# The first two heads of a cross-attention and feed-forward kernel in true fp32 products

## The chip, the cores and the metric

The kernel runs on one core of one Trainium2 chip. The metric is the device time of one execution in microseconds, the median of the runs shown. Durations come from one profiled execution; their times are counted from the start of its span.

## The reference

Two residual blocks follow one another on `x` of shape (2, 512, 512), fp32. Cut to what matters:

```python
h    = layernorm(x)
q_hk = (h @ Wq.T).reshape(B, S, 16, 128)                # "down"
q_big = einsum('bshk,hkq->bshq', q_hk, w_kc_q)          # "up", 384 wide
q_big = q_big * cos + rotate_half(q_big) * sin
q_r  = einsum('bshq,hqr->bhsr', q_big, W_qr)            # rank 64
k_r  = einsum('bld,hdr->bhlr', rope(ctx), W_kr)         # ctx: (2, 1024, 128)
attn = softmax(q_r @ k_r.T)
x    = x + ((attn @ rope(ctx)) @ w_kc_kv.T).reshape(B, S, 2048) @ Wo.T
y    = layernorm(x)
x    = x + bit_linear(silu(bit_linear(y, gate)) * bit_linear(y, val), out)
```

`bit_linear` rounds its input to 8-bit levels and its weight to -1, 0, 1 times a mean. All inputs are fp32. The scores are sharp, so the chain from `h` to `q_r` has to keep more than a 16-bit product gives.

## The kernel before, in words

The attention runs in 32 steps `i`, one for a head and a batch. `STEPS` orders them: step 0 is head 0 of batch 0, step 1 head 1 of batch 0, steps 2 and 3 the same heads of batch 1, then heads 2 and 3, and so on. A weight is prepared once for a head `u` and serves two steps.

Precision is kept by pairs of parts. The weight of a head (`rawa`, 128 rows, 896 columns of down and up weights and 192 of the rank projection) is scaled by a power of two and split into two fp16 parts, `whi` and `wlo`. The normalized input `hid` is turned by TensorE and split into two fp16 parts (`hid_part`). A product is then three fp16 matmuls: high by high, high by low, low by high. In front of the split stand `w_mass` (a bound on the weight's size), `w_bound` (a matmul that spreads it over the partitions), `w_factor` (the power of two), `w_scale`, `w_hi`, `w_lo`. For the first two heads (`FIRST = 2`) ScalarE does the mass, the scaling and the high part; for the others VectorE and GpSimd do. The rank weight is split into two parts of the reduced fp32 type `F32R` (`wr_hi`, `wr_lo`) that lie side by side.

A step passes through these functions:

- `q_down`: four chunks of the 512-wide contraction, three fp16 matmuls each (L603), into one PSUM bank.
- `q_hi` (ScalarE, L610) and `q_lo` (VectorE, L614): the two fp16 parts of the result.
- `q_up`: three blocks of 128 columns, three fp16 matmuls each (L622).
- `rot_copy`, `rot_half` (ScalarE), `rot_cos` (VectorE), `rot_sin`, `rot_add` (GpSimd): the rotation.
- `rot_hi` (ScalarE, L646) and `rot_lo` (GpSimd, L650): two F32R parts of each rotated block.
- `q_rank`: three blocks, two F32R matmuls each (L657). The two halves of its output hold the products with the high and the low part of the rank weight.
- `t_hi` twice (ScalarE, L665), `t_res` (L671) and `t_lo` (L676, both VectorE): the query in two F32R parts, scaled back.
- `score` (L717), `s_max` (L721), `s_exp` (L725), `s_scale`, `s_recip`, `e_hi` (L737), `e_lo` (L742), `e_turn` (a transposing DMA), `mix` (L757), `project` (L775): scores, softmax, weighted context and output.

Beside the steps run the table and context work of the start (`kv_*`, `val_*`, `load_*`), the keys (`key_*`), and the quantization of the feed-forward weights (`w_sum`, `w_round`, `w_tern`, `w_store`), which reads its input twice. The feed-forward stage (`ff_*`) follows when attention ends; its weights lie in buffers with the tags `ffg` and `ffv`, which nothing else uses before.

The order of all work is written out by hand in the table `ISSUE`: each function has a tuple of places, one for each call. The calls are sorted by place and issued in that order, and each engine, the DMA queue of SyncE included, works through its own instructions strictly in it. Before the first real work, TensorE runs idle products of an identity (L464, fp32, 12 of them) and of a wide tile (L470).

Of the kernel before, what the change touches and what calls it, by code (L numbers as in the profile page):

```python
# [13 lines left out]
F32 = mybir.dt.float32  # L14
# [19 lines left out]

HIDS = 2.0 ** 10

FIRST = 2


def qscale(u):  # L40
    return 2.0 ** -14 if u < FIRST else 2.0 ** -16
# [18 lines left out]
        528, 577, 582, 537, 766, 775, 761, 745, 962, 1087, 1050, 994, 1164, 1175, 1198, 1213, 1450, 1418, 1479, 1411,  # L60
        1623, 1626, 1598, 1573, 1879, 1869, 1806, 1823, 2030, 2002, 2013, 2059, 2293, 2272, 2306, 2373, 2501, 2464,
        2524, 2476, 2727, 2718, 2647, 2774, 2849, 2857, 2907, 2932, 3102, 3131, 3044, 3050, 3298, 3236, 3284, 3229,
        3353, 3356, 3397, 3411, 3487, 3505, 3526, 3538,
    ),
    "b_hi": (144, 220, 533, 784, 876, 1189, 1405, 1645, 1883, 2046, 2266, 2509, 2770, 2862, 3079, 3270),
    "b_lo": (163, 226, 556, 798, 892, 1190, 1413, 1658, 1934, 2065, 2342, 2516, 2771, 2872, 3100, 3272),
    "c_hi": (
        402, 489, 649, 729, 859, 948, 1077, 1151, 1261, 1358, 1446, 1537, 1679, 1783, 1913, 1983, 2145, 2228, 2374,
        2418, 2547, 2623, 2757, 2835, 2936, 3021, 3139, 3220, 3324, 3344, 3426, 3483,
    ),  # L70
    "c_lo": (
        408, 490, 662, 731, 866, 950, 1080, 1152, 1276, 1378, 1470, 1538, 1703, 1797, 1914, 1988, 2187, 2246, 2375,
        2420, 2548, 2628, 2758, 2836, 2937, 3022, 3150, 3223, 3325, 3345, 3475, 3484,
    ),
    "e_hi": (
        225, 258, 280, 300, 324, 352, 394, 407, 476, 442, 500, 535, 562, 586, 611, 631, 645, 663, 706, 739, 759, 772,
        797, 826, 847, 870, 905, 927, 951, 982, 997, 1028, 1048, 1076, 1097, 1123, 1142, 1179, 1202, 1211, 1240, 1262,
        1311, 1326, 1361, 1399, 1407, 1440, 1445, 1491, 1507, 1535, 1559, 1582, 1616, 1646, 1666, 1687, 1725, 1768,
        1764, 1831, 1834, 1872, 1884, 1942, 1943, 1994, 2023, 2042, 2091, 2095, 2128, 2134, 2182, 2202, 2249, 2242,
        2295, 2297, 2332, 2349, 2390, 2400, 2426, 2450, 2478, 2507, 2530, 2557, 2580, 2602, 2627, 2650, 2684, 2710,  # L80
        2723, 2754, 2780, 2794, 2841, 2843, 2889, 2913, 2931, 2994, 3009, 2973, 3053, 3043, 3095, 3086, 3126, 3144,
        3178, 3204, 3226, 3241, 3253, 3286, 3306, 3312, 3346, 3366, 3385, 3395, 3423, 3437,
    ),
    "e_lo": (
        236, 265, 285, 310, 329, 353, 404, 409, 480, 445, 501, 545, 572, 587, 612, 633, 654, 685, 720, 740, 760, 778,
        811, 830, 857, 877, 911, 931, 960, 983, 998, 1032, 1054, 1078, 1098, 1124, 1144, 1180, 1203, 1222, 1246, 1263,
        1312, 1343, 1375, 1400, 1416, 1461, 1463, 1505, 1508, 1536, 1565, 1585, 1619, 1654, 1673, 1689, 1735, 1772,
        1771, 1835, 1837, 1877, 1890, 1945, 1949, 2007, 2024, 2045, 2092, 2096, 2131, 2161, 2186, 2203, 2253, 2250,
        2296, 2298, 2333, 2362, 2391, 2404, 2427, 2469, 2482, 2508, 2535, 2558, 2591, 2608, 2638, 2653, 2691, 2715,
        2732, 2755, 2795, 2800, 2855, 2856, 2892, 2922, 2934, 3006, 3015, 2976, 3065, 3054, 3111, 3087, 3127, 3165,  # L90
        3183, 3210, 3228, 3242, 3279, 3287, 3308, 3320, 3349, 3375, 3389, 3399, 3425, 3441,
    ),
    "e_turn": (
        257, 276, 336, 337, 373, 374, 454, 457, 486, 532, 522, 546, 664, 665, 690, 691, 704, 719, 747, 750, 777, 782,
        831, 848, 858, 878, 930, 932, 987, 1007, 1038, 1052, 1075, 1079, 1137, 1181, 1194, 1214, 1223, 1299, 1308,
        1309, 1350, 1376, 1448, 1449, 1466, 1520, 1499, 1550, 1553, 1570, 1649, 1667, 1683, 1717, 1753, 1754, 1786,
        1827, 1858, 1859, 1870, 1880, 1908, 1946, 1987, 2100, 2055, 2056, 2102, 2139, 2152, 2194, 2221, 2263, 2264,
        2365, 2307, 2336, 2385, 2402, 2424, 2425, 2444, 2521, 2540, 2541, 2565, 2594, 2617, 2667, 2701, 2707, 2742,
        2744, 2769, 2773, 2817, 2822, 2881, 2897, 2903, 2986, 2999, 3080, 3083, 3099, 3113, 3114, 3137, 3153, 3181,
        3187, 3193, 3256, 3277, 3278, 3288, 3289, 3334, 3342, 3372, 3386, 3390, 3400, 3463, 3464,  # L100
    ),
    "ff_center": (3378, 3368, 3434, 3438, 3521, 3520, 3567, 3570),
    "ff_end": (3677, 3725, 3809, 3766, 3847, 3854, 3862, 3865),
    "ff_gate": (
        3443, 3447, 3460, 3469, 3516, 3522, 3534, 3498, 3573, 3555, 3547, 3586, 3620, 3609, 3594, 3629, 3649, 3658,
        3666, 3641, 3692, 3717, 3707, 3674, 3737, 3760, 3723, 3759, 3777, 3791, 3797, 3824,
    ),
    "ff_hint": (
        3513, 3515, 3539, 3540, 3600, 3623, 3601, 3619, 3636, 3668, 3679, 3655, 3698, 3701, 3699, 3713, 3720, 3770,
        3732, 3788, 3787, 3807, 3790, 3795, 3818, 3823, 3819, 3822, 3840, 3841, 3845, 3849,  # L110
    ),
    "ff_hmax": (
        3479, 3481, 3486, 3488, 3563, 3564, 3565, 3572, 3603, 3616, 3617, 3631, 3656, 3663, 3664, 3670, 3680, 3704,
        3710, 3712, 3728, 3731, 3754, 3755, 3769, 3773, 3782, 3785, 3813, 3821, 3832, 3836,
    ),
    "ff_hround": (
        3502, 3506, 3508, 3509, 3576, 3611, 3575, 3618, 3635, 3667, 3678, 3637, 3693, 3684, 3691, 3705, 3718, 3746,
        3730, 3784, 3761, 3757, 3758, 3792, 3808, 3806, 3804, 3820, 3838, 3839, 3844, 3843,
    ),
    "ff_hscale": (3501, 3574, 3634, 3675, 3715, 3756, 3786, 3837),  # L120
    "ff_hturn": (3541, 3646, 3727, 3742, 3799, 3810, 3825, 3842, 3850),
    "ff_in": (
        3435, 3436, 3445, 3446, 3448, 3450, 3458, 3459, 3503, 3504, 3510, 3511, 3518, 3523, 3492, 3493, 3557, 3558,
        3553, 3554, 3535, 3542, 3584, 3585, 3599, 3602, 3589, 3590, 3587, 3588, 3615, 3622, 3647, 3648, 3652, 3653,
        3654, 3665, 3639, 3640, 3688, 3689, 3711, 3716, 3696, 3697, 3669, 3673, 3734, 3735, 3743, 3745, 3721, 3722,
        3736, 3741, 3762, 3763, 3779, 3783, 3774, 3775, 3802, 3803,
    ),
    "ff_int": (3404, 3406, 3473, 3490, 3559, 3597, 3628, 3671),
    "ff_max": (3379, 3382, 3439, 3452, 3530, 3531, 3591, 3592),
    "ff_out": (  # L130
        3560, 3577, 3578, 3581, 3685, 3695, 3702, 3703, 3729, 3789, 3800, 3801, 3748, 3749, 3751, 3752, 3815, 3816,
        3817, 3846, 3828, 3829, 3833, 3834, 3848, 3852, 3853, 3856, 3858, 3859, 3860, 3864,
    ),
    "ff_prod": (
        3462, 3466, 3468, 3472, 3533, 3537, 3546, 3507, 3583, 3571, 3562, 3598, 3626, 3613, 3614, 3633, 3657, 3662,
        3687, 3645, 3706, 3726, 3738, 3683, 3768, 3772, 3767, 3781, 3812, 3814, 3831, 3835,
    ),
    "ff_residual": (3497, 3431, 3500, 3457, 3740, 3851, 3861, 3659),
    "ff_round": (3403, 3402, 3454, 3489, 3552, 3595, 3627, 3621),
    "ff_scales": (3401, 3453, 3536, 3606),  # L140
    "ff_silu": (
        3444, 3449, 3465, 3470, 3532, 3524, 3543, 3499, 3579, 3556, 3561, 3596, 3625, 3610, 3607, 3630, 3650, 3660,
        3686, 3642, 3694, 3724, 3709, 3682, 3744, 3771, 3747, 3780, 3798, 3805, 3811, 3830,
    ),
    "ff_store": (3796, 3753, 3827, 3776, 3857, 3855, 3863, 3866),
    "ff_turn": (3405, 3456, 3474, 3529, 3638, 3604, 3643, 3690),
    "ff_value": (
        3442, 3451, 3461, 3471, 3512, 3527, 3544, 3494, 3582, 3569, 3548, 3593, 3624, 3612, 3605, 3632, 3651, 3661,
        3672, 3644, 3700, 3719, 3708, 3676, 3739, 3765, 3733, 3764, 3778, 3793, 3794, 3826,
    ),  # L150
    "ff_vbias": (3467, 3545, 3549, 3608, 3681, 3714, 3750),
    "hid_norm": (7, 8, 33, 26, 126, 128, 152, 156),
    "hid_part": (25, 27, 36, 37, 46, 47, 41, 42, 138, 154, 140, 146, 167, 168, 177, 183),
    "hid_turn": (9, 24, 45, 31, 130, 129, 159, 176),
    "key_hi": (
        71, 88, 272, 331, 477, 543, 641, 681, 937, 963, 1110, 1125, 1279, 1296, 1427, 1513, 1738, 1775, 1915, 1958,
        2166, 2177, 2352, 2392, 2485, 2578, 2730, 2813, 2992, 3030, 3162, 3200,
# [16 lines left out]
    ),  # L174
    "kv_add": (35, 64, 135, 210),
    "kv_cos": (34, 55, 107, 155),
    "kv_hi": (56, 67, 182, 253),
    "kv_lo": (60, 68, 197, 273),
    "kv_sin": (32, 50, 122, 196),
    "ln_eps": (4, 14, 106, 127),  # L180
# [1095 lines left out]
```

## Time and profile before

| | before |
|---|---|
| median of 3 runs | 776.47 us (775.09 to 776.72) |
| profiled execution, its own time | 773.01 us |
| its span | 771.2 us |
| mean granted TensorE clock | 0.987 |
| TensorE busy | 727.8 us (94%) |
| VectorE busy | 706.4 us (92%) |
| ScalarE busy | 671.5 us (87%) |
| GpSimd busy | 603.0 us (78%) |
| DMA | 145.28 MB, mean 188 GB/s |

An engine's share is an average over the start, the 32 steps and the feed-forward stage. Matmuls are pipelined: a row of the trace gives a 512-column fp16 matmul 0.38 us from start to end, while the next one starts 0.216 us after it. Work on TensorE is counted by the second number.

### The profile page before, as it was taken

What the parts mean: (1) busy time and instruction counts of PE and PEld (TensorE: products, weight loads), DVE (VectorE), ACT (ScalarE), POOL (GpSimd) and SP (SyncE); (2) the same over time, 40 slices, a digit from 0 to 9 for tenths busy, and PEclk for the clock granted to TensorE, in tenths of its full rate; (3) what the DMA queues carried; (4) which work ended last, traced back from release to release, by engine and by line L of the source; (5) the groups of instructions that cost most, each with busy time, mean ns of one, the idle gap of its engine ahead of it and who ended that gap; (6) DMA issues with size and microseconds to landing.
All of it is one profiled execution on the core that took longest, in us unless ns stands there. A gap on an engine that the chain in (4) does not pass through costs nothing. (4 is left out here: it accounts for less than half of the span.)

```text
span 771.2 us, 12603 instructions
## 1 busy us (share of the span) xinstructions
PE 727.8 (94%) x3949; PEld 479.9 (62%) x3958; DVE 706.4 (92%) x1255; ACT 671.5 (87%) x1110; POOL 603.0 (78%) x599
## 2 busy tenths in 40 slices
PE   6767999999999998999999999999999998899998
PEld 5333765666676665666766677777766776553443
DVE  6899999999999898989898999999999999999995
ACT  6698999999998998999999999998898987766873
POOL 3889998788787777898898888897987763379972
PEclk8798999999999999999999999999999999999999
DMA  8635878899999989999999989999999899843354
GB/s 257 204 115 113 187 169 178 192 189 230 209 207 208 226 204 212 213 236 212 214 224 213 207 172 228 198 220 200 201 255 179 183 202 211 157 125 69 69 119 127
DMA packets 326083, 145.28 MB, mean 188 GB/s; under 512 B 291968, under 2 KB 299136, under 8 KB 325760
## 3 DMA queue, kind: packets, MB, share of 16 engines
q1 hardware_dynamic: 326016, 144.48, 85.5%
q8 instruction: 31, 0.51, 0.3%
q14 instruction: 36, 0.29, 0.1%
HBM read 55.31 MB, written 8.39 MB: 83 GB/s over the span
## 5 line engine op out<-in xcount | busy, mean ns | idle before, releaser
L757 PE MATMUL mps<-et,kvh 128*128 128x256 f16 x1024 | 174.8, 273 | 2.2 <-DMA et<-e 1.9
L742 DVE SCALAR_TENSOR_TENSOR e<-sc,m,e 128x1024 f16<-128x1024 f32 x128 | 163.1, 1278 | 8.4 <-ACT e L737 6.9
L721 DVE TENSOR_REDUCE m<-sc 128x1 f32<-128x1024 f32 x128 | 155.4, 1217 | 8.7 <-PE sc L717 7.3
L737 ACT ACTIVATE e<-sc,m 128x1024 f16<-128x1024 f32 x128 | 142.2, 1116 | 17.0 <-ACT sc L725 7.3
L650 POOL TENSOR_TENSOR l<-u,h 128x512 fp32r<-128x512 f32 x96 | 123.8, 1290 | 42.4 <-ACT h L646 25.6
L725 ACT ACTIVATE sc<-sc,m 128x1024 f32<-128x1024 f32 x128 | 139.4, 1089 | 8.2 <-DVE m L721 7.0
L639 POOL TENSOR_TENSOR c<-c,sinq 128x512 f32<-128x512 f32 x96 | 123.5, 1288 | 23.5 <-ACT c L626 13.7
L757 PE MATMUL mps<-et,kvl 128*128 128x256 f16 x512 | 139.6, 273 | 0.0
L642 POOL TENSOR_TENSOR u<-u,c 128x512 f32<-128x512 f32 x96 | 122.7, 1282 | 11.7 <-DVE u L636 6.6
L757 PEld LDWEIGHTS <-kvh 128*128 128x128 f16 x1024 | 94.4, 98 | 40.2 <-issue 20.8
L603 PE MATMUL qps<-hid,whi 128*128 128x512 f16 x256 | 80.6, 397 | 5.5 <-DVE am L967 2.0
L717 PE MATMUL sc<-ko,t 128*128 128x512 f32 x256 | 75.5, 416 | 7.3 <-DVE e L742 2.7
L717 PE MATMUL sc<-ke,t 128*128 128x512 f32 x256 | 75.2, 416 | 4.2 <-DVE e L742 2.5
L636 DVE TENSOR_TENSOR u<-ups,cosq 128x512 f32<-128x512 f32 x96 | 65.2, 681 | 2.9 <-POOL l L650 1.5
L646 ACT CAST h<-u 128x512 fp32r<-128x512 f32 x96 | 59.0, 620 | 4.2 <-POOL u L642 3.8
L717 PEld LDWEIGHTS sc<-ko,t 128*128 128x128 f32 x256 | 44.3, 188 | 26.6 <-issue 4.7
L717 PEld LDWEIGHTS sc<-ke,t 128*128 128x128 f32 x256 | 45.0, 189 | 20.4 <-issue 5.8
L775 PE MATMUL pps<-woh,ch 128*128 128x512 f32 x128 | 54.0, 421 | 0.0
L603 PE MATMUL qps<-hid,wlo 128*128 128x512 f16 x128 | 50.6, 395 | 3.3 <-POOL wlo L554 3.3
L757 PEld LDWEIGHTS <-kvl 128*128 128x128 f16 x512 | 50.1, 98 | 5.7
L775 PE MATMUL pps<-woh,cl 128*128 128x512 f32 x128 | 50.6, 395 | 0.4 <-DVE cl L765 0.3
L775 PE MATMUL pps<-wol,ch 128*128 128x512 f32 x128 | 50.1, 392 | 0.0
(168 smaller groups left out, 1645.9 us busy)
## 6 DMA issues: line engine op xcount, KB each, us to landing
rawa<-in_wall SPq DMA_DIRECT2D x16, 544.0 KB, 4.5
fd<-fo SPq DMA_DIRECT2D x48, 128.0 KB, 3.0
rawb<-in_wall SPq DMA_DIRECT2D x16, 320.0 KB, 3.8
fs<-in_fg SPq DMA_DIRECT2D x16, 256.0 KB, 3.2
ke<-kl SPq DMA_DIRECT2D x32, 128.0 KB, 3.2
ko<-kl SPq DMA_DIRECT2D x32, 128.0 KB, 3.2
ft<-in_fg SPq DMA_DIRECT2D x16, 256.0 KB, 3.4
fs<-in_fv SPq DMA_DIRECT2D x16, 256.0 KB, 3.6
```

What stands on the lines that cost most here:

```text
L603: nc.tensor.matmul(qs[i][0], lhsT=a[:, c * K:(c + 1) * K], rhs=hidp[b][:, m, c, :], start=c == 0 and n == 0, stop=c == 3 and n == 2,)
L636: nc.vector.tensor_tensor(us[i, j], up[i, j], cosq[:, j, :], ALU.mult)
L639: nc.gpsimd.tensor_tensor(cs[i, j], cs[i, j], sinq[:, j, :], ALU.mult)
L642: nc.gpsimd.tensor_tensor(us[i, j], us[i, j], cs.pop((i, j)), ALU.add)
L650: nc.gpsimd.tensor_tensor(ls[i, j], us.pop((i, j)), sb(hs[i, j]), ALU.subtract)
L717: nc.tensor.matmul(ps[:, block(c)], lhsT=a[:, rows], rhs=keys[i][:, block(c)], start=n == 0, stop=n == 1)
L721: nc.vector.tensor_reduce(m[:, 0:1], sc[i, st], AX.X, ALU.max, negate=True)
L725: nc.scalar.activation(ps, ps, AF.Exp, bias=m[:, 0:1], accum_out=m[:, 1:2])
L737: nc.scalar.activation(e[:, 0, :], sc[i, st], AF.Copy, scale=sm[i, st][:, 2:3])
L742: nc.vector.scalar_tensor_tensor(e[:, 1, :], sc.pop((i, st)), m[:, 2:3], e[:, 0, :], ALU.mult, ALU.subtract)
L757: nc.tensor.matmul(ps, lhsT=a[:, b, c, :], rhs=et[:, m + c, :], start=c == 0 and n == 0, stop=c == 7 and n == 2)
L775: nc.tensor.matmul(ps, lhsT=a[:, rows], rhs=w, start=m == 0, stop=m == 5)
```

## The change

For heads 0 and 1, that is for steps 0 to 3 (`FULL = 4`), the chain from the normalized input to the rank projection works on plain fp32 operands:

- `load_a` of these heads loads only the 896 columns of down and up weights, into one fp32 tile with the tag `ffv`. Mass, bound, factor, scaling and split of these two weights are gone.
- `wr_hi` becomes two DMAs that put the rank weight into both halves of an fp32 tile; `wr_lo` is gone for these heads.
- A new step `hid_full` copies each turned block of the input to an fp32 tile with the tag `ffg` (ScalarE, eight calls). The fp16 parts of the input are still made for the other heads.
- `q_down`, `q_up` and `q_rank` issue one fp32 matmul where they issued three, three and two.
- `q_hi` becomes a plain copy; `q_lo`, `rot_hi`, `rot_lo`, the second `t_hi` and `t_lo` are gone in these steps; `t_hi` and `t_res` work on all 128 rows.
- The whole table `ISSUE` is new. The list has 3,825 calls instead of 3,867.

In the diff, cut to its core (the tuples of `ISSUE` are left out):

```diff
 HIDS = 2.0 ** 10
+QS = 2.0 ** -16
 FIRST = 2
-def qscale(u):
-    return 2.0 ** -14 if u < FIRST else 2.0 ** -16
+FULL = 2 * FIRST
...
     def load_a(u):
+        if u >= FIRST:
+            raw[u, 0] = const.tile([P, WB], F32, tag="rawa", name=f"rawa{u}")
+            nc.sync.dma_start(raw[u, 0], wall[SPLITS[u], :, 0:WB])
+            return
+        if not u in wsp:
+            both = const.tile([P, FIRST, WA], F32, tag="ffv", name="rawf")
+            for k in range(FIRST):
+                wsp[k] = [both[:, k, :]]
+        nc.sync.dma_start(wsp[u][0], wall[SPLITS[u], :, 0:WA])
...
     def wr_hi(u):
+        if u < FIRST:
+            w = wsp[u, 2] = wspl.tile([P, 3, 2 * R], F32, tag="wr", name=f"wr{u}")
+            for e in range(2):
+                nc.sync.dma_start(w[:, :, half(e)], wall[SPLITS[u], :, WA:WB].rearrange("p (c r) -> p c r", c=3))
+            return
...
     def q_down(i, c):
+        if i < FULL:
+            w = wsp[SPLIT[i]][0]
+            nc.tensor.matmul(qs[i][0], lhsT=w[:, c * K:(c + 1) * K], rhs=hidf[0][:, b, c, :], start=c == 0, stop=c == 3)
+            return
...
     def q_hi(i):
+        if i < FULL:
+            qs[i].append(lp.tile([P, S], F32, tag="l", name=f"qf{i}"))
+            nc.scalar.copy(qs[i][1], qs[i][0])
+            return
...
     def q_up(i, j):
+        if i < FULL:
+            nc.tensor.matmul(ps, lhsT=wsp[SPLIT[i]][0][:, wc], rhs=qs[i][1], start=True, stop=True)
+            return
...
     def rot_cos(i, j):
-        us[i, j] = up_.tile([P, S], F32, tag="u", name=f"u{i}_{j}")
+        n, tag = (hp, "h") if i < FULL else (up_, "u")
+        us[i, j] = n.tile([P, S], F32, tag=tag, name=f"u{i}_{j}")
...
     def q_rank(i, n):
+        if i < FULL:
+            nc.tensor.matmul(rs[i], lhsT=wsp[SPLIT[i], 2][:, j, :], rhs=us.pop((i, j)), start=n == 0, stop=n == 2)
+            return
...
     def t_hi(i, n):
+        if i < FULL:
+            nc.scalar.copy(ts[i][0], rs[i])
+            return
...
     def t_res(i):
+        if i < FULL:
+            nc.vector.tensor_tensor(ts[i][1], rs[i], sb(ts[i][0]), ALU.subtract)
+            return
...
+    def hid_full(t):
+        if not hidf:
+            hidf[0] = const.tile([P, B, 4, S], F32, tag="ffg", name="hidf")
+        b, cols = t // 4, slice(t % 4 * P, (t % 4 + 1) * P)
+        nc.scalar.copy(hidf[0][:, b, :, cols], hps[t].rearrange("p (c s) -> p c s", c=4))
```

In the new order the first 30 entries of TensorE are: the turns 0, 3, 2, 1, the first key block, `q_down` of step 0, `q_up` of step 0 (with the second key block and one turn of the context among them), `q_down` of step 1, turns 4 and 5, one `q_up` of step 1, the three `q_rank` of step 0 (with turn 7 among them), the rest of `q_up` of step 1, turn 6, the first score. Before, turn 6, turn 7 and two turns of the context stood among or ahead of the same steps. `load_a` of head 0 was the sixth load call of SyncE's queue; it is now the fifteenth, behind seven of the eight blocks of `x` (256 KB each), two blocks of the context with their swapped copies (256 KB each), both tables (512 KB each) and a key weight (64 KB). From the first `mix` on the two orders differ by local exchanges: a call's distance from the end of the list changes by some 15 places on average.

## The prediction

> **What bounds the kernel now.** I read the page first (busy shares, slices), then a table by stages, then the waits of TensorE in the start, then single rows. The page's slices:
>
> ```profile
> PE   6767999999999998999999999999999998899998
> DVE  6899999999999898989898999999999999999995
> PEclk8798999999999999999999999999999999999999
> ```
>
> TensorE is short of work only in the first four slices (77 us) and a little near the end; VectorE is full from the second slice on. The table by stages cuts at the first matmul of `q_down` (16.55 us), at the first usable score (49.5), at the first `mix` (83.0) and near the end of attention (640). The numbers behind an engine are busy us and instructions; behind the last engine stand granted clock, DMA share and GB/s.
>
> ```profile
> core 0: us, PE busy (x) PEld busy (x) DVE busy (x) ACT busy (x) POOL busy (x), PEclk, DMA share, GB/s
> 0.00:16.55 16.55, 11.01 (x61) 9.13 (x61) 10.26 (x39) 11.57 (x19) 3.82 (x13) 0.91 0.86 268
> 16.55:22.14 5.59, 5.34 (x15) 2.10 (x15) 3.95 (x7) 1.30 (x4) 4.68 (x4) 0.64 0.84 295
> 22.14:49.50 27.36, 17.04 (x71) 8.73 (x69) 26.14 (x59) 21.45 (x42) 23.32 (x20) 0.88 0.53 161
> 49.50:83.00 33.50, 27.25 (x111) 15.34 (x112) 32.55 (x53) 30.39 (x54) 30.66 (x26) 0.90 0.48 106
> 83.00:640.00 557.00, 548.46 (x3115) 382.12 (x3114) 516.82 (x824) 520.04 (x866) 455.79 (x419) 1.00 0.97 206
> ```
>
> From 83 to 640 us TensorE works 548.5 of 557 us at full clock: there, time is TensorE's work. Between 22 and 83 VectorE works 58.7 of 60.9 us, and TensorE waits. So the start is worth what VectorE's queue can be shortened by, and a microsecond of TensorE costs something only behind the first `mix`. The waits of TensorE between 16 and 83 us say the same: a late `wlo`, and results of VectorE.
>
> ```profile
> PE rps L657 <- DVE hid L901: 3.3, 1, 3.3
> PE qps L603 <- POOL wlo L554: 3.3, 1, 3.3
> PE sc L717 <- DVE e L742: 2.1, 1, 2.1
> PE qps L603 <- DVE am L967: 2.0, 1, 2.0
> ```
>
> **The change, queue by queue, up to the first `mix`.** I count what each issue list has ahead of the first `mix`, each call at the mean of its row.
>
> *VectorE.* Gone: four `q_lo` of 0.69 (2.8), two of the `t_lo` of 0.75 that stood ahead of that point (1.5), two `w_factor` of three 0.15 us instructions (0.9); three `t_res` at 0.68 instead of 0.75 (0.2). By the new order one `s_max` and one `e_lo` of step 1 fall behind the first `mix` and one `rot_cos` comes ahead of it (1.8). Together 7.2: from 73.0 us to 65.8. The row 73.0 fits the table, whose stages up to 83 us add to 72.9.
>
> *ScalarE.* Gone: mass, scale and high part of two weights (6.2), two `wr_hi` (0.7), 11 `rot_hi` of 0.62 (6.8), three second `t_hi` (2.0), 0.2 on the others, one `e_hi` by order (1.1). Added: eight `hid_full`, at the 0.59 of `hid_part` (4.7), and two `rot_half` by order (1.2). From 70.6 to 59.4.
>
> *GpSimd.* Gone: 11 `rot_lo` of 1.285 (14.1) and `w_lo`, `wr_lo` and the small product of two weights (5.4); one `rot_sin` more. From 66.3 to 48.1.
>
> *TensorE.* Before, a step costs 12 and 9 fp16 matmuls at 0.216 and 6 F32R matmuls at 0.231: 5.9 us. After, it costs ten fp32 products of 512 columns, which this trace does not have. The nearest rows are the idle products at the start, 12 in the code and 24 in the trace:
>
> ```profile
> 1.36 5.49 PE L464 MATMUL warm<-ident 128*128 128x128 f32 x24 [1.36 <-POOL ident masks.py:199]
> ...
> L464 PEld LDWEIGHTS warm<-ident x24: 286/333/333, 1.4 to 6.2; 128*128 128x128 f32 x24
> ```
>
> An fp32 product is two instructions. If each streamed its columns once, a product would cost 2 x 0.231 = 0.46 us; if these rows scale with the columns (5.19 us of loads over 12 products, times 4), 1.73. The median load of such a block takes 333 ns, that of an F32R block of the same size 188 (L717), so I take two passes for each instruction: 4 x 0.216 = 0.86 us, between the ends. The Trainium skill speaks against the change here ("FP8 and Floating Point Precision", TensorE Precision Notes): true fp32 takes four passes where the pairs take three or two. No run here shows that price; by it the sum is the one that I make. Ten products are 8.6 us a step, 2.7 more than before, 10.7 over four steps. Ahead of the first `mix` lie 37 of the 40, and two `w_bound` go: from 39.6 us to 48.9.
>
> **When the first `mix` comes.** *Its beginning does not move.* `load_a` of head 0 now stands behind 4.0 MB instead of 1.3; with its own 0.46 MB, and at the 268 GB/s of the first stage, it lands at 16.6 us, about where `q_down` starts now. The new DMAs, two for each rank weight, stand in SyncE's queue ahead of a context block and two loads; four issues at the 0.5 us of `load_swapped` are 2 us in a queue that was empty from 22.4 to 31.6, and they pass under the rotation of step 0. I cost them at nothing; without that cover it is 2 us.
>
> *The chain of step 0.* At the half clock that the second stage starts with, two products take 1.72 us each, then two 0.86: 5.2 us, against 4.9 now from `q_down` to `q_hi` (21.49). `q_up` has no `q_lo` to wait for, so its first block ends where it does now, near 23.4. Then GpSimd no longer stands in the way: of the 22.7 us that it has ahead of the first `q_rank`, 11.8 go. VectorE has 33.5 us ahead of the first score instead of 38.0, so I expect that score 4.5 us sooner by VectorE alone, and up to 6.5 with less stretching (below).
>
> *The stage.* With VectorE as full as now, the first `mix` comes 7.2 us sooner, at 75.8. For TensorE that leaves 59.2 us from 16.6 on, for 46.6 us of work (48.9 less what lies ahead of `q_down`). It may lose 12.6 us, where it loses 28.6 now (66.5 less 37.9). Of these, 3.3 are the wait for `wlo`, which is gone, and 6.7 half clock (the clock's shortfall times TensorE's busy time in three stages), which denser work shortens.
>
> Two things bound that 7.2. The 1.8 by order are work put off, not saved: at worst they come back, and the shift is 5.4. On the other side VectorE's rows are stretched beside GpSimd's, and GpSimd has 18 us less to do:
>
> ```profile
> 30.38 1.87 DVE L854 SCALAR_TENSOR_TENSOR ln<-ln 128x1 f32<-128x1 f32 x2
> ...
> 64.36 3.96 DVE L938 TENSOR_TENSOR ktl<-kvt,kth 128x512 fp32r<-128x512 f32 x1
> ```
>
> Elsewhere these take 0.23 us for the two and 0.68; GpSimd ran tensor-tensor instructions through both. The four `ktl` rows at a mean of 1.90 give 4.9 us, and the `ln` and `kvt` rows of the start bring it to some 10; a third of that gone would make the shift 10.5.
>
> Behind the first `mix` TensorE has three fp32 products of `q_rank` more, 3 x (0.86 - 0.46) = 1.2 us, at full price. **Sum: -7.2 + 1.2 = -6.0 us.** Against the profiled execution (773.0 us, span 771.2 and 1.8 around it) that is 767.0; the median lies 3.5 above that execution, so 770.5. Own range: -9.3 with less stretching, -4.2 when the order gives nothing, and 1 us for 557 us of shuffled order: 766 to 773.5.
>
> **Rivals.** *TensorE becomes the bound of the start (slower).* It loses 28.6 us now. If only the waits for `wlo` and the 3.3 us wait at the first `rps` go, 22.0 stay, since turns, products and scores stand in one strict queue and each longer product holds up what is behind it. Then the first `mix` comes at 16.6 + 46.6 + 22.0 = 85.2, 2.2 later than now, and with the 1.2 behind it the time is 779.9. It decides from a loss of 18.6 us on. For it: 37 longer products in the stretch with the poorest clock. Against: the present waits are for VectorE and GpSimd, which get shorter queues. The clock has a rule: after the 3.3 us wait for `wlo` the granted clock is 0.50 from 31 to 35 us. The Trainium skill ("TensorE: Matmul & The Clock Gate", Part 1) puts it as an activity window of about 3.4 us that halves the clock; the trace agrees. Long fp32 products keep TensorE busy, so by that rule the rival is less likely.
>
> *The fp32 product costs 1.73 us.* Then 46.6 becomes 78.8, the first `mix` comes at 105 even with only 10 us lost, and with 3.8 behind it the time is about 803. For it: the plain scaling of the only fp32 row. Against: that row has loads as long as its products.
>
> *No difference: the gain is lost in the order.* TensorE idles 8.5 us between 83 and 640; should the new order add 6 us there, or the first fp32 weight land 6 us late, the time stays at 776.5. For it: every call has a new place. Against: the places differ by local exchanges only.
>
> **How the numbers follow.** Forecast 0.64, TensorE as the bound 0.20, no difference 0.11, the dear product 0.05. The range of 765.5 to 780.5 takes in the forecast, its rival on the other side and no change, and leaves out the dear product and the tails. A measurement can tell about 0.2% (1.6 us) from no change. Faster gets the forecast and 0.03 of the lighter ends of the others, 0.67; the same 0.08; slower the rest, 0.25.
>
> **What would show it.** Right: the fp32 records of `q_down` 0.43 us from start to start at full clock; no `wlo` row for heads 0 and 1; the first usable score at 43 to 45 us, the first `mix` at 74 to 77, VectorE full between them; and 83 to 640 as dense as now. Wrong: a first `mix` at or after 82, TensorE full from 40 us on while VectorE waits, or fp32 rows of 0.8 us from start to start.

## The result and the profile after

The changed kernel took 765.49 us (763.16 to 768.17, four runs), the kernel before 775.78 on the same chip: a ratio of 0.9867, with a 95% interval of 0.9840 to 0.9894. Three later comparisons gave 0.9913 [0.9898, 0.9928], 0.9890 [0.9870, 0.9909] and 0.9912 [0.9884, 0.9941]. By medians the gain is 10.3, 6.8, 8.2 and 7.9 us. The execution first profiled, 763.16 us with a span of 761.4, is the fastest of the changed kernel's.

The page's slices after the change, for TensorE, VectorE and the granted clock:

```profile
PE   6899999999999999999999999999999998899997
DVE  6789999999999999989899998999999999999995
PEclk8899999999999999999999999999999999999999
```

TensorE, which was short of work in the first four slices, is now short in two. The table by stages, at the cuts of the prediction:

```profile
core 0: us, PE busy (x) PEld busy (x) DVE busy (x) ACT busy (x) POOL busy (x), PEclk, DMA share, GB/s
0.00:16.55 16.55, 11.12 (x59) 9.48 (x60) 9.94 (x38) 9.18 (x15) 3.06 (x12) 0.89 0.85 271
16.55:22.14 5.59, 4.80 (x8) 1.91 (x7) 4.72 (x10) 3.47 (x7) 3.10 (x3) 0.50 1.02 405
22.14:49.50 27.36, 22.97 (x69) 11.33 (x68) 22.30 (x50) 18.70 (x36) 16.02 (x14) 0.92 0.49 138
49.50:83.00 33.50, 33.42 (x143) 19.92 (x142) 30.60 (x60) 30.23 (x55) 29.89 (x27) 1.00 0.69 156
83.00:640.00 557.00, 550.05 (x3114) 384.31 (x3112) 518.54 (x822) 519.37 (x864) 447.85 (x411) 1.00 0.99 206
```

Read the fourth row first. From 49.5 to 83 us TensorE is busy for 33.42 of 33.50 us (27.25 before), while VectorE, full before, has gaps: 30.60 there and 22.30 of 27.36 in the row above. From 40 us to the first `mix` TensorE is busy for 36.06 of 36.14 us. The full engine of the start is now TensorE, and still the first `mix` comes at 76.14 us instead of 82.98. The waits of TensorE between 16 and 83 us are short now; the wait for `wlo` is gone, and the longest is for block 7 of the input:

```profile
PE hidps L912 <- ACT hid L907: 2.5, 1, 2.5
PE kps L708 <- ACT wk L699: 1.2, 1, 1.2
PE qps L600 <- ACT hidf L920: 0.8, 1, 0.8
```

Rows of `q_down` in the timeline (start, us, and in brackets the idle time before):

```profile
18.48 5.96 PE L600 MATMUL qps<-hidf,rawf 128*128 128x512 f32 x8 [0.79 <-ACT hidf L920]
29.34 3.60 PE L600 MATMUL qps<-hidf,rawf 128*128 128x512 f32 x8
```

Four products are eight records; the last record is 0.59 us long, so at full clock they start (3.60 - 0.59) / 7 = 0.43 us apart, and a product costs 0.86. The first row runs partly at half clock, which is granted from 12.8 to 23.1 us.

Where the 9.8 us between the two profiled spans lie, by the first `mix` and the first `mix` of the last step:

| profiled execution | first `mix` | from there to the last step's | from there to the end | span |
|---|---|---|---|---|
| before | 82.98 | 585.7 | 102.5 | 771.2 |
| before again | 82.82 | 585.5 | 102.5 | 770.8 |
| after | 76.14 | 585.5 | 99.7 | 761.4 |
| after again | 77.04 | 589.3 | 99.7 | 766.1 |
| after, third | 76.20 | 589.0 | 99.8 | 765.0 |
| after, fourth | 76.25 | 588.2 | 99.7 | 764.2 |

By these columns the start gives 6.5 us in the mean of four and the end 2.8; the attention between them takes 0 to 3.7 us more. But the cut between the two middle columns has moved. The new order puts eight products of the feed-forward stage (1.7 us) ahead of the last step's first `mix`; before, none stood there. First the kernel before, then the changed one:

```profile
668.70 0.39 PE L757 MATMUL mps<-et,kvh 128*128 128x256 f16 x2 [1.28 <-DMA et<-e]
```

```profile
659.93 1.02 PE L1090 MATMUL gv<-ffg,fqt 128*128 128x512 bf16 x4 [1.37 <-DVE e L760]
660.79 1.03 PE L1090 MATMUL gv<-ffv,fqt 128*128 128x512 bf16 x4
661.66 0.38 PE L775 MATMUL mps<-et,kvh 128*128 128x256 f16 x2
```

With these products counted where the old order has them, the end gives 1.1 us, and the attention takes between 1.8 us less and 2.0 us more. "Stretch" below is all that lies behind the first `mix`, the two middle columns together; the moved cut does not touch it.

### The profile page after: what moved, and what is told of

It is laid out like the page before. It is cut to its first block, busy times and chain, and to the rows that moved or that the text cites. A ratio compares the mean times of both kernels' runs of the same rounds, so it can differ in the third digit from the quotient of the medians.

```text
span 761.4 us, 12487 instructions
## 1 busy us (share of the span) xinstructions
PE 732.5 (96%) x3926; PEld 483.8 (64%) x3926; DVE 694.4 (91%) x1241; ACT 659.6 (87%) x1092; POOL 580.1 (76%) x581
## 5 line engine op out<-in xcount | busy, mean ns | idle before, releaser
L659 POOL TENSOR_TENSOR l<-u,h 128x512 fp32r<-128x512 f32 x84 | 107.1, 1278 | 47.2 <-ACT h L655 32.9
L651 POOL TENSOR_TENSOR u<-u,c 128x512 f32<-128x512 f32 x96 | 122.7, 1283 | 11.9 <-DVE u L645 6.2
L604 PE MATMUL qps<-hid,whi 128*128 128x512 f16 x224 | 66.9, 380 | 0.6 <-DVE u L645 0.6
L735 PEld LDWEIGHTS sc<-ke,t 128*128 128x128 f32 x256 | 45.0, 188 | 17.9 <-issue 4.4
L655 ACT CAST h<-u 128x512 fp32r<-128x512 f32 x84 | 51.9, 622 | 2.2 <-POOL u L651 2.0
L832 POOL TENSOR_SCALAR ft<-ft,fgw 128x512 f32<-128x512 f32 x48 | 33.3, 695 | 22.4 <-DMA ft<-in_fv 7.3
```

Of the source, the lines that this page charges most:

```text
L604: nc.tensor.matmul(qs[i][0], lhsT=a[:, c * K:(c + 1) * K], rhs=hidp[b][:, m, c, :], start=c == 0 and n == 0, stop=c == 3 and n == 2,)
L651: nc.gpsimd.tensor_tensor(us[i, j], us[i, j], cs.pop((i, j)), ALU.add)
L659: nc.gpsimd.tensor_tensor(ls[i, j], us.pop((i, j)), sb(hs[i, j]), ALU.subtract)
L735: nc.tensor.matmul(ps[:, block(c)], lhsT=a[:, rows], rhs=keys[i][:, block(c)], start=n == 0, stop=n == 1)
```

## The experiments

**The two kernels again.** No edit.

> The kernel before, unchanged, for a second profile of it. The changed kernel ran twice, with 685.3 and 689.0 us behind its first mix, so one profile of the kernel before does not tell what its stretch behind the first mix (688.2) is worth. Theory 1 (the step of 1.2 us more work behind the first mix was right, and the first profile of the changed kernel was a lucky execution): 687 to 689 again. Theory 2 (the kernel before scatters as much): 684 or 692.

Measured: one execution of 772.57 us; first `mix` at 82.82, stretch 687.98.

> The changed kernel unchanged, as the yardstick for the runs beside it. Both theories: a ratio to before near 0.987, some 765.5 us.

Measured: 767.75 us against 774.59; first `mix` 77.04, stretch 689.02.

> The changed kernel unchanged, a third time, as the yardstick on this chip. Its stretch behind the first mix took 685.3 and 689.0 us in two profiles; the kernel before took 688.2 and 688.0. Theory 1 (the stretch scatters by some 2 us about 687 in the new order): 685 to 689, ratio to before 0.987 to 0.991. Theory 2 (one of the two profiles is an outlier): within 0.5 us of one of them, and the ratio with it.

Measured: 766.78 against 774.98; first `mix` 76.20, stretch 688.79.

> The changed kernel once more. Its stretch from the first `mix` to the end was 685.24, 689.02 and 688.79 us in three profiled executions. Theory 1 (the time depends on when the feed-forward blocks that ScalarE sums up land behind the transposes in SyncE's queue; late by a microsecond is the usual case): 688 to 690 us, an execution of 766 to 768, and the wait of ScalarE for such blocks is 4 to 6 us in sum. Theory 2 (685 is the usual case and the other two were disturbed by half clock and the chip): 684.5 to 686, an execution near 763, and these waits sum to 2 us.

Measured: 765.94 against 773.87; first `mix` 76.25, stretch 687.95; ScalarE's waits for feed-forward blocks sum to 3.6 us. Stretches of 688 to 689 are the usual case; the 685.24 of the first profile was the favourable one.

**Which engine sets the first `mix`.** One engine's queue is made longer or shorter in steps 0 to 3.

```diff
 rot_cos (extra VectorE, +8.2 us)
+        for _ in range(2 if i < FULL else 1):
             nc.vector.tensor_tensor(us[i, j], up[i, j], cosq[:, j, :], ALU.mult)
 q_up (extra TensorE, +10.3 us)
+            for _ in range(2):
                 nc.tensor.matmul(ps, lhsT=wsp[SPLIT[i]][0][:, wc], rhs=qs[i][1], start=True, stop=True)
 q_down (half of it, -6.9 us)
+            if c in (1, 2): return
```

> The changed kernel with each rot_cos of steps 0 to 3 issued twice: 12 x 0.68 = 8.2 us more for VectorE ahead of the first mix, nothing else. Theory 1 (TensorE sets the first mix: it is full from 40 us on, VectorE idles some 8 us between 22 and 83): 1 to 4 us slower than the changed kernel. Theory 2 (VectorE sets it, as the prediction counted): 7 to 8 us slower.

Measured: 769.34 us; first `mix` 80.47.

> The changed kernel with each q_up of steps 0 to 3 issued twice: 12 fp32 products more, 10.3 us of TensorE, some 8 of them behind 40 us. Theory 1 (TensorE sets the first mix): 7 to 10 us slower than the changed kernel. Theory 2 (VectorE sets it and TensorE has 11 us to lose): 0 to 3 us slower.

Measured: 771.02 us; first `mix` 83.14. From 49.5 to 83 us TensorE has no gap left:

```profile
49.50:83.00 33.50, 33.50 (x109) 17.70 (x107) 27.70 (x49) 27.86 (x50) 25.26 (x23) 1.00 0.55 112
```

> The changed kernel with two of the four chunks of q_down left out in steps 0 to 3, so that part of the contraction is missing: 8 fp32 products less, 6.9 us of TensorE. Theory 1 (TensorE sets the first mix): 4 to 7 us faster than the changed kernel, first mix at 70 to 73. Theory 2 (VectorE sets it): at most 1.5 us faster.

Measured: 760.34 us; first `mix` 72.89. Against the usual 76.2, VectorE's 8.2 us cost 4.3, TensorE's 10.3 cost 6.9, and TensorE's 6.9 taken away gave 3.3. Neither engine sets the start alone: of an added microsecond, half to two thirds arrive at the first `mix`, TensorE's more than VectorE's (the clock's part in these figures is taken out further below).

**The code without the order.** The changed code is issued in the order of before (`hid_full` just ahead of its `hid_part`); then the new order up to the first `mix` with the old one behind it. Only the places in `ISSUE` differ.

> The changed code in the issue order of before: the calls that the change drops are left out of the old list, and each hid_full stands just ahead of its hid_part. Theory 1 (the gain is fp32 code that shortens the element-wise queues, so the first mix comes earlier in any order): the first mix 4 to 7 us earlier than before (76 to 79 us), the time 768 to 772, since the 1.2 us of q_rank and the old order's gaps stay. Theory 2 (the new list of places makes the gain, the code only allows it): the first mix at 81 us or later, the time 775 or more.

Measured: 776.44 us against 774.59, a ratio of 1.0027 [1.0010, 1.0044]; first `mix` 81.38, stretch 690.78. TensorE's waits from 16 to 83 us:

```profile
PE hidps L672 <- ACT hid L667: 3.6, 1, 3.6
PE kps L468 <- DVE ktl L724: 2.3, 1, 2.3
PE sc L495 <- DVE e L520: 2.0, 1, 2.0
```

Up to the first `mix` VectorE now has 61.5 us of work instead of 72.9 and GpSimd 46.3 instead of 62.5, and yet nothing is gained: `q_down` begins at 14.10 us, but TensorE then stands in its strict queue at the low part of the first key, at the turns of blocks 4 and 5 and at a score. Of these two orders, only the new one uses the freed time. The reverse, the new order with the old code, was not run. In the kernel before, VectorE has 62.6 us of work between 16.55 us and the first `mix`, of which the new order puts 1.8 off; by that estimate its first `mix` could not come before 77.4 us if VectorE's rows keep their length, even with VectorE never idle. How much the order would bring without the code is open. The stretch, 2.7 us longer than before's, fits the code's added work behind the first `mix`, but one profile is no more than the scatter.

> The changed code; up to the first mix the new order, behind it the old order. Behind its first mix the changed kernel took 685.3 us in the profile and the one before 688.2, though 1.2 us of work were added. Theory 1 (the 4.2 us are the new order's, behind the first mix): the first mix at 76 us as in the changed kernel, then 689 us, the time 768 to 770. Theory 2 (they are carried over from the start: shorter queues of VectorE and ScalarE leave TensorE fewer gaps later): 684 to 686 us behind the first mix, the time 764 to 766.

Measured: 768.95 us; first `mix` 77.11, stretch 689.65, of which 586.2 in attention and 103.4 at the end. With the old order behind the first `mix`, the end takes 103.4 and 103.8 us (this kernel and the one above); with the new order it takes 99.5 to 100.1 in all sixteen other profiles of the changed code, of which 1.7 us are the eight products that have moved ahead of the cut. So with the changed code the new order shortens the end by some 2 us, in every profile. Against the kernel before it is 1.1 us, of which 0.9 is idle time of TensorE behind the last `mix`. The 1.28 us wait for a transposed block in the row of the kernel before lies ahead of the cut and is no part of the end.

**The clock in the start.** In all four profiles of the changed kernel block 7 is waited for by some 2.5 us and half clock follows. The edits move calls: the key weight and the first fp32 weight are loaded earlier, and block 7 is turned later (shown at their new places only).

```diff
 order of the calls
+load_wk(0)
 load_ctx(1)
...
+load_a(0)
 load_x(4)
...
 q_rank(0, 2)
+t_hi(0, 0)
+hid_turn(7)
+hid_full(7)
+hid_part(7, 0)
```

> The changed kernel with two moves in its start: the key weight and the first fp32 weight are loaded earlier in SyncE's queue, and the turn of input block 7 stands behind the three q_rank of step 0 instead of among them (its copies behind the t_hi). In the changed kernel ScalarE waited 1.2 us for the key weight and TensorE 2.5 us for block 7. Theory 1 (TensorE is full from 40 us on, so its lost time ahead of that counts in full): the first mix 2.5 to 3.7 us earlier, the time 762 to 763. Theory 2 (VectorE sets the first mix): the same first mix within 1 us, the time unchanged.

Measured, with all of it: 761.87 us, a ratio of 0.9835 [0.9817, 0.9853]; `q_down` at 17.58, first `mix` at 72.93, half clock only up to 20.9.

> The changed kernel with only the second of the two moves: the turn of input block 7 behind the three q_rank of step 0, its copies behind t_hi; the loads as they were. Both moves together gave 4.1 us at the first mix. Theory 1 (the 2.5 us wait for block 7 counts, and with it the half clock that followed from 40.1 to 43.6 us, 1.7 us of TensorE's work): 2.5 to 4 us faster than the changed kernel, no half clock behind 25 us. Theory 2 (the earlier start of q_down is what counts, the wait only changes its place): 0 to 1 us faster.

Measured, with the turn alone: 764.88 us against 774.98; no half clock near 40 us, but up to 25.4; first `mix` 76.21.

> The changed kernel with the two weight loads earlier (key weights ahead of the second context block, the first fp32 weights ahead of the fifth input block) and the turn of block 7 where it stood. Theory 1 (the gain of the tightened start came from the loads): q_down begins near 17.6, the first score is used near 42.5, the first `mix` comes at 72.9 to 73.6 and the time is 4 to 6 us under the changed kernel's. Theory 2 (each alone is worth little, since the other wait then ends last): q_down begins near 17.6, block 7 is still waited for with TensorE idle and half clock follows near 40 us, first `mix` 74.5 to 76.2, time 0 to 2 us under.

Measured, with the loads alone: 763.25 us against 773.87; `q_down` at 17.88, half clock to 22.6 and again from 39.7 to 43.1; first `mix` 75.41. In its profile each part alone is worth little at the first `mix`. In time the parts gave 1.9 us (turn) and 2.7 us (loads) against the changed kernel's medians on the same chips, and both together 5.9. With the loads alone six executions took 760.78 to 768.26 us, and the profiled one, at 765.51, is among the slower, so its first `mix` need not be the usual one. The next test fills TensorE with idle products behind three turns, on top of the tightened start.

```diff
 hid_turn
+        keep_warm({0: 14, 3: 8, 1: 10}.get(t, 0))
```

> The tightened kernel with idle products of the wide tile behind the turns 0, 3 and 1 of the start (14, 8 and 10 of them, some 0.11 us each), so that TensorE has no long gaps between 9 and 17 us. In the tightened kernel the clock is 0.5 from 12.8 to 23 us and q_down of step 0 takes 5.3 us instead of 3.4. Theory 1 (the half clock there lies on the path to the first mix): the clock at 1.00 through q_down, first mix 1.5 to 2.5 us earlier than 72.9, the time 759.5 to 760.5. Theory 2 (other engines' results set the first score, q_down then only waits later): less than 0.7 us.

Measured: 762.40 us against 774.98; first `mix` 73.02. `q_down` of step 0 ran at full clock, 3.70 us instead of 5.34, and half clock came from 34.0 to 37.4 instead.

All these executions fall on one line. With T from the start of `q_down` to the first `mix`, and C the half clock within it:

| kernel | `q_down` | C | first `mix` | T |
|---|---|---|---|---|
| after (four executions) | 18.48 to 18.89 | 7.2 to 9.2 | 76.14 to 77.04 | 57.4 to 58.5 |
| loads only | 17.88 | 8.2 | 75.41 | 57.5 |
| turn only | 19.26 | 6.2 | 76.21 | 57.0 |
| tightened | 17.58 | 3.3 | 72.93 | 55.4 |
| tightened, kept warm | 17.70 | 3.4 | 73.02 | 55.3 |
| second block buffer (below) | 18.65 | 0.0 | 72.36 | 53.7 |
| both (below) | 17.32 | 0.7 | 71.25 | 53.9 |

A straight line through these and the four other kernels that leave the work of the start alone, 14 executions in all, is T = 53.6 + 0.505 C, and none lies more than 0.26 us off it. Half of the half clock is lost, and the rest of the chain takes 53.6 us in these executions. C was not set by hand, with one exception that fits: the idle products made `q_down` 1.6 us shorter, C stayed the same because half clock came later, and so did T. The tightened start owes about 1 of its 3.3 us to the earlier `q_down` and 2.3 to less half clock. Against this line, and so freed of the clock, VectorE's added 8.2 us cost 5.4, TensorE's 10.3 cost 7.9, and TensorE's 6.9 taken away gave 3.5. The Trainium skill reckons alike ("TensorE: Matmul & The Clock Gate", Part 1: half of the throttled time is added, and the activity window runs freely, so that its place differs from run to run); the slope of 0.505 and the 0 to 9.2 us of C here agree. The row that decides is block 7's turn; first the changed kernel, then the kernel with the second block buffer (C = 0), whose start is the same program:

```profile
39.67 0.71 PE L912 MATMUL hidps<-ident,hid 128*128 128x128 f32 x4 [2.50 <-ACT hid L907]
```

```profile
37.57 0.66 PE L912 MATMUL hidps<-ident,hid 128*128 128x128 f32 x4 [1.85 <-ACT hid L907]
```

After 2.50 us idle (2.62 in the fourth profile) the clock was half for 3.4 us; after 1.85 it stayed full.

**Behind the first `mix`: the price of work.** Each `q_up` of steps 4 to 7 is computed twice, 36 fp16 matmuls or 7.8 us.

```diff
 q_up
+        for _ in range(2 if i < 2 * FULL else 1):
```

> The changed kernel with each q_up of steps 4 to 7 issued twice: 36 fp16 matmuls of 0.216, 7.8 us of TensorE, nearly all behind the first mix; the start is unchanged. Theory 1 (behind the first mix a microsecond of TensorE costs one, as the prediction priced the 1.2 us of q_rank): 7 to 8 us slower than the changed kernel. Theory 2 (the stretch has slack that takes such work up, which would also explain its scatter): 2 to 5 us slower.

Measured: 773.55 us against 766.78 for the changed kernel on that chip; stretch 695.66. 6.8 of 7.8 us arrive: behind the first `mix` TensorE's work costs nearly its full length.

**Behind the first `mix`: the scatter.** The first and third profile of the same program part by 1.2 us at 125 us, at one row of ScalarE, the sum over a feed-forward block. First the first profile, then the third:

```profile
123.80 0.63 ACT L810 ACTIVATE fs<-fs 128x512 f32<-128x512 f32 x1 [1.07 <-DMA fs<-in_fg]
```

```profile
125.03 0.63 ACT L810 ACTIVATE fs<-fs 128x512 f32<-128x512 f32 x1 [2.22 <-DMA fs<-in_fg]
```

The load was issued at 120.66 and at 121.56 us, behind transposes and key moves in SyncE's queue. So 26 of the 48 sums were issued one or two `e_hi` later, in the changed kernel and with the tightened start:

```diff
 order of the calls, for f from 10 to 39
-w_sum(f)
 e_hi(i)
 e_hi(i + 1)
+w_sum(f)
```

> The changed kernel, with 26 of the 48 sums over feed-forward blocks issued behind one or two more probability parts on ScalarE, so that ScalarE takes the score chain first and finds its block landed; the loads stand where they stood. Theory 1 (the scatter behind the first `mix` comes through these waits): ScalarE's waits for these blocks in the moved places fall from 4 to 6 us to under 1, the stretch behind the first `mix` is 685 to 687 us in every execution, and the time is 763.5 to 765.5, under the changed kernel's on the same chip by 1.5 to 3 us. Theory 2 (the waits are only where the lag shows; SyncE's queue or TensorE sets it): the waits vanish and the stretch stays at 688 to 690, the time within 1 us of the changed kernel's. Theory 3 (each later sum holds up the next load): slower by 1 to 3 us.

Measured: 815.38 us, a ratio of 1.0532 [1.0504, 1.0561]; stretch 737.01.

> The tightened start (both loads earlier, block 7's turn later) together with the later sums. Theory 1 (they add up): first `mix` at 73, stretch 685 to 686, time 758.5 to 761. Theory 2 (the stretch does not follow the sums): 761.5 to 763, as with the tightened start alone.

Measured: 808.39 us; stretch 732.72. The reverse of the hope, at a price that none of the theories had. Theory 3 of the first of these two runs had named the way, with 1 to 3 us. The blocks share one buffer, so that the next load waits for the sum at the head of SyncE's queue, and transposes and key moves stand behind it. SyncE's own waits, in the fourth profile of the changed kernel and then with the sums later (us, times, longest):

```profile
SPq L804 <- ACT fs L810: 25.8, 15, 6.7
```

```profile
SPq L564 <- ACT fs L570: 86.8, 28, 6.9
```

61 us more at the head of the queue went with a stretch 49 us longer; behind the first `mix` alone the wait is 72.6 us against 11.8. Of the 49 us, 35 are idle time of TensorE, and some 12 are half clock (27.3 us of it against 4.2, half of it lost). ScalarE's wait for the transposes to free its probabilities grew from 1.4 to 16.0 us, as the queue would have it. That the queue is the whole route is argued, not shown: the later sums also changed ScalarE's order, and they were not run with a second buffer.

In the changed kernel's own four profiles the wait behind the first `mix` is 8.3, 9.0, 8.4 and 11.8 us, while the stretch is 685.24, 689.02, 688.79 and 687.95. So the wait does not follow the scatter. The last two runs shorten the wait without moving a sum or its load: every second block goes into the buffer of the fp32 input, free by then.

```diff
-        fs[f] = const.tile([P, FP], F32, tag="fs", name=f"fs{f}")
+        fs[f] = const.tile([P, FP], F32, tag="ffg" if f > 8 and f % 2 else "fs", name=f"fs{f}")
```

> The changed kernel in its own order, with every second feed-forward block from the tenth on loaded into a buffer that is free in that time (that of the normalized input in fp32), so that a load no longer waits for the sum over the block before it. In the changed kernel SyncE waited 22.7 to 25.8 us for these sums, and with the sums issued later 86.8 us, the stretch behind the first `mix` being 685 to 689 and 737. Theory 1 (the stretch follows SyncE's waits in front of the transposes): SyncE's wait for ScalarE's sums falls to under 7 us, the stretch is 683 to 686 and the time 761 to 764, under the changed kernel's usual 766 by 2 to 5 us. Theory 2 (only waits beyond those of the changed kernel cost; these lie beside other waits of the queue): the wait falls and the stretch stays at 687 to 689, the time within 1 us of 766.

Measured: 764.47 us against 773.86, a ratio of 0.9888 [0.9861, 0.9916]; stretch 687.06, SyncE's wait 11.9 in all and 1.8 behind the first `mix`. The first `mix` at 72.36 belongs to the clock (C = 0), since the edit touches nothing of that time. The profiled execution, 761.23 us, is the fastest of four, and the other three took 763.66 to 765.62.

> The tightened start together with the second block buffer. Theory 1: first `mix` at 73, stretch 683 to 686, time 757 to 760. Theory 2: first `mix` at 73, stretch 686 to 689, time 761 to 763, as with the tightened start alone.

Measured: 759.12 us (758.06 to 759.86), a ratio of 0.9813 [0.9791, 0.9835]; first `mix` 71.25, stretch 684.95. This is the fastest version, 14.7 us under the kernel before on its chip. Where the wait is short, taking it away went with a stretch 1 to 2 us shorter (687.06 against the usual 687.95 to 689.02; 684.95 against 686.73), less than the width of the scatter: one profile each doesn't show that more than luck is in it. Where it was made long, four fifths of its length came back as time.

## Why the prediction was right and wrong, step by step

*The price of an fp32 product* was right: 0.43 us from start to start, 0.86 a product, which is four times the 0.216 of an fp16 matmul. The trace so agrees with the rule of four passes in the Trainium skill ("FP8 and Floating Point Precision", TensorE Precision Notes).

*The beginning* was off by 2 us. `q_down` starts at 18.5 us, not 16.6: ScalarE's queue, which the prediction had not followed to that point, brings the fp32 copies late, behind a wait for the key weight. With the loads earlier it starts at 17.9. The first usable score came at 45.65, just past the forecast's 43 to 45.

*The first `mix`* was right in its number (75.8 forecast, 76.14 to 77.04 measured) by a reason that does not hold. "VectorE full between them" failed, and the sign named for the forecast's fall, TensorE full from 40 us on while VectorE waits, appeared. That the two numbers agree is in part luck. The rival took TensorE as the bound to mean a first `mix` at 85.2, because it kept 22 us of losses; TensorE lost 57.7 - 46.6 = 11.1 us, within the 12.6 that the forecast allowed. So TensorE became a bound, and it was a faster one. Of the 11.1 us, 4 are half clock. (The half clock that the prediction puts at 31 to 35 us in the kernel before ran from 30.8 to 37.6 and began while TensorE still waited for `wlo`.)

*What VectorE's shorter queue is worth* was mis-stated. The queue shrank by more than the 7.2 us of the sum: up to the first `mix` VectorE's work fell from 72.9 to 61.0 us, because the stretched rows, which the sum left to the low end of the range, shrank too (the four `ktl` rows from 7.6 to 3.0 us). Yet in the old order, with 61.5 us of work, the first `mix` comes 1.6 us sooner and no time is gained. The new places, which the prediction booked as 1.8 us put off and otherwise as neutral, were needed to turn free engines into an earlier `mix`.

*The stretch behind the first `mix`* is the step that failed, in its size. The prediction had three fp32 products at full price, 1.2 us, and "1 us for 557 us of shuffled order"; the end had no term. The price of work held (6.8 of 7.8 us). But the new order is not neutral: with the changed code it shortens the end by some 2 us, 1.1 us against the kernel before. And the attention part scatters by 3.8 us between executions of one program. So the stretch, forecast at +1.2, was -2.9 in the first profile and -0.2 to +0.9 in the other three. With the eight moved products in their old place the mean of four is -6.5 for the start, +0.7 for the attention and -1.1 for the end, or -6.9, where the forecast said -6.0.

Of the 5.0 us between 770.5 and 765.49, the stretch makes 4.2 (-3.0 between the two first profiles, instead of +1.2) and the step from the profiled execution to the median 1.2 (2.3 us instead of 3.5); the start takes 0.4 back. Scatter decides here: 765.49 lies 0.01 us under the low end of the range, and the medians of the three later runs, 765.94 to 767.75, lie above it. The order should have had some 3 us to either side instead of 1, and the end a term of its own.

*The rivals.* The fp32 product at 1.73 us and "no difference" did not occur. "The gain is lost in the order" is what the changed code does in the old order.

*What stays open*: what decides between 585.5 and 589.3 us of attention. TensorE's idle time there is 12.5, 13.9, 14.9 and 13.2 us in the four profiles. The second and the fourth also hold 3.4 us of half clock near 650 us, worth up to 1.7 us. The rest is not explained. One jump was followed to a late block; taking away the wait that precedes such loads moved the stretch by no more than the scatter. Open too is what the new order would do without the code.

## What to carry to other kernels

When a change shortens the queue of the full engine, look at the next engine's work plus its losses in the same stage, and price them as a second bound: here both stood within a few microseconds, and each added microsecond counted half to three quarters. In a hand-issued kernel the order is a part of the change with its own account, stage by stage, the end included; and where a stage is cut at a call, look which work the new order has carried across the cut. And a load at the head of a shared DMA queue that waits for its buffer is a wait of everything behind it: moving its consumer later lengthened that wait by 61 us here and the kernel by 49.

## What the hardware showed beyond the forecast

Half clock came in stretches of 3.4, 6.8, 10.2 and 13.6 us, and the same start got 0 to 9.2 us of it between `q_down` and the first `mix`, from execution to execution. An idle gap of 2.50 us, shorter than the shortest of these stretches, was followed by 3.4 us of half clock; one of 1.85 us was not. Each microsecond of half clock cost 0.505 us of a start that TensorE fills.
